# First image's loads spread over three queues, identity products at the start, and one weight's quarters issued by GpSimd

## The chip, the cores and the metric

The kernel runs on one core of a Trainium2 chip. The core has TensorE (PE: matrix products; its weight loads are listed as PEld), VectorE (DVE), ScalarE (ACT), GpSimd (POOL) and SyncE (SP). Each engine works through its own instructions in order. Transfers between memory and the core's buffers are issued by SyncE, ScalarE or GpSimd and carried out by 16 DMA engines. The metric is the device time in microseconds (us) of one execution, the median of several.

## The reference

The input x holds 8 images of 32 x 32 pixels with 512 channels, in float32. Two layers are computed.

1. An attention layer. Each image (1024 tokens of 512 channels) is group-normalized in groups of 16 channels, multiplied by a 512 x 1536 matrix w_qkv to give queries, keys and values, put through softmax attention with 8 heads of 64, multiplied by w_out, and added to x.
2. A deformable attention layer. The result is layer-normalized, projected (wq), put through a 7 x 7 depthwise convolution of stride 2, a GELU and a small projection that gives offsets; at the offset positions the input is sampled bilinearly (256 samples), keys and values are made of the samples by products of weights (wv with mk and mv), the 1024 queries attend to the 256 samples, and an output projection, a layer norm and an MLP with GELU follow.

In the first layer what matters here is:

```python
x_norm = _group_norm(x, gn_scale, gn_bias).reshape(b, seq, c)
qkv = x_norm @ w_qkv + b_qkv
...
out = out @ w_out + b_out
return (x_flat + out).reshape(b, h, w, c)
```

## The kernel before

**Order of the work.** The class `InOrder` keeps every engine's instructions in the order in which the program issues them. That order is written out by hand: `at(place, step)` notes a step with a place, a number in units, and `run_due(until)` issues all noted steps below a place, smallest first. One unit is one tile of 128 queries for one pair of heads: scores, their softmax, and the products with the values. An image has 4 pairs of heads with 8 tiles, so 32 units (`per`); eight images make 256. All instructions of the first layer carry one line in the profile (L54, the helper's), so they are told apart by the names of their tiles.

**The start.** The 8 tiles of the first image, 128 tokens by 512 channels each (256 KB), are loaded before anything else: tiles 0 to 3 by GpSimd, tiles 4 to 7 by SyncE. SyncE then issues three small vectors (gsc, gbi, bqkv, laid onto partitions element by element), the three thirds of w_qkv, 1 MB each, in the order wB (keys), wA (queries), wC (values), and three rows. `norm_steps(0, -100, ...)` notes the first image's steps: `turn(t)` transposes tile t on TensorE by four products with the identity matrix `ident` into a PSUM tile (tag mm, three buffers) and copies it by ScalarE into xT; `two_tiles` takes the statistics of two tiles on VectorE (four instructions); then come the group means, the deviations, a power on GpSimd, the factors, and `norm`, which scales xT in place on VectorE and ScalarE. Between these stand two calls of `warm(3)`, six products of `ident` with xT whose result is not read. Then the first key projection reads wB. After each of the first two transposes, `turn` issues a load of a tile of the next image (`load_x`, two buffers) on GpSimd; w_out is loaded by GpSimd after the first image's normalization, by `load_weight`.

**Scores on their way.** In each unit the exponentials e are transposed by blocks on VectorE into sq; after every second unit `MovedAttention.moved` issues 16 transfers of 128 KB on SyncE that carry sq into et, with the partitions exchanged. Two units later, `part` multiplies et with the values (av). `share` and `spread` send the reciprocal sums through memory and back (rs_d, inv).

**The last image.** Beside the attention of the last image, `fold_steps` multiplies weights of the second layer with each other (wv with mk and mv, wq with mq), and so loads more weights. There is one buffer w of 1 MB for w_out, wq and wv in turn. After wv has been transposed out of it, `load_quarter` fetches w_out for the last image in four quarters of 256 KB at units 25.2, 25.7, 26.2 and 26.7 of that image, issued by ScalarE. Quarters of mv follow at 27.2, 27.9, 28.6 and 29.3 into another buffer (raw), also by ScalarE. The last image's output products (mm<-w,attT) read w_out.

Of the kernel before, what the change touches and what calls it, by code (L numbers as in the profile page):

```python
# [17 lines left out]
P = 128  # L18
# [3 lines left out]
C = 512  # L22
# [4 lines left out]
NQT = QB // P  # L27
NH = 8
HD = 64
# [219 lines left out]
def attention_then_deformable_attention(  # L249
# [30 lines left out]
    nc = tc.nc  # L280
    x_tok = x.rearrange("b h w c -> b (h w) c")
# [8 lines left out]
    ident = const.tile([P, P], F32, tag="ident", name="ident")  # L290
# [7 lines left out]
    def mm_tile():  # L298
        return ps_mm.tile([P, QB], F32, tag="mm", name="mm")

    def by_chunk(w):
        return w.rearrange("(c p) o -> p c o", p=P)
# [6 lines left out]
    def load_cols(pool, v, name):  # L309
        t = pool.tile([P, v.shape[0] // P], F32, tag=name, name=name)  # L310
        with nc.allow_non_contiguous_dma(reason="a vector onto partitions"):
            nc.sync.dma_start(t, v.rearrange("(c p) -> p c", p=P))
        return t

    def load_row(pool, v, name):
        t = pool.tile([P, C], F32, tag=name, name=name)
        nc.sync.dma_start(t, v.partition_broadcast(P))
        return t
# [49 lines left out]
    def at(place, step):  # L368
        due.append((place, len(due), step))
# [40 lines left out]
    def kept(name):  # L410
        return keep.tile([P, NC, C], F32, tag=name, name=name)
# [98 lines left out]
    with ExitStack() as l0:  # L510
# [3 lines left out]
        nc = InOrder(tc)  # L514
        NX = 2
        NX_T = 3
        xs = {}

        def load_x(b, t):
            if b < B:  # L520
                xs[b, t] = work.tile([P, C], F32, tag="x", name="x", bufs=NX)
                nc.gpsimd.dma_start(xs[b, t], x_tok[b][ts(t, P), :])
# [2 lines left out]
        x2 = work.tile([P, NC, QB], F32, tag="xT", name="x2", bufs=NX_T)  # L525
        for t in range(NQT):
            xs[0, t] = work.tile([P, C], F32, tag="attT", name="x0", bufs=NQB * NHP)
            nc.gpsimd.dma_start(xs[0, t], x_tok[0][ts(t, P), :])
            xs[0, NQT + t] = x2[:, t, :]
            nc.sync.dma_start(xs[0, NQT + t], x_tok[0][ts(NQT + t, P), :])  # L530
        w3 = [kept(name) for name in ("wA", "wB", "wC")]
        gsc = load_cols(wp, gn_scale, "gsc")
        gbi = load_cols(wp, gn_bias, "gbi")
        bqkv = load_cols(wp, b_qkv, "bqkv")
        for i in (1, 0, 2):
            nc.sync.dma_start(w3[i], by_chunk(w_qkv)[:, :, ts(i, C)])
        bout = load_row(wp, b_out, "bout")
        room_w = {}

        def load_weight(w):  # L540

            room_w["w"] = work.tile([P, NC, C], F32, tag="w", name="w", bufs=1)
            nc.gpsimd.dma_start(room_w["w"], by_chunk(w))

        def load_quarter(w, c):
            if c == 0:
                room_w["w"] = work.tile([P, NC, C], F32, tag="w", name="w", bufs=1)
            nc.scalar.dma_start(room_w["w"][:, c, :], by_chunk(w)[:, c, :])

        lng_row = load_row(wp, ln_g, "lng_row")  # L550
        lnb_row = load_row(wp, ln_b, "lnb_row")
# [7 lines left out]
            out=g3, in_=g3, pattern=[[-GRP, ng], [0, GRP]], compare_op=ALU.is_ge,  # L559
# [3 lines left out]
            out=g3, in_=g3, pattern=[[GRP, ng], [0, GRP]], compare_op=ALU.is_ge,  # L563
# [5 lines left out]
        def norm_steps(b, start, places):  # L569

            room = {}

            def turn(t):
                blk, i = divmod(t, NQT)
                if i == 0:
                    xTs[b, blk] = work.tile([P, NC, QB], F32, tag="xT", name="xT", bufs=NX_T)
                if t == 0:
                    room["stats"] = work.tile([P, NC, NT // 2, 6], F32, tag="stats", name="stats", bufs=1)
                ps = mm_tile()
                for c in range(NC):  # L580
                    nc.tensor.transpose(ps[:, ts(c, P)], xs[b, t][:, ts(c, P)], ident)
                nc.scalar.copy(xTs[b, blk][:, :, ts(i, P)], ps.rearrange("p (c q) -> p c q", q=P))
                if b > 0:
                    load_x(b + (t + NX) // NT, (t + NX) % NT)
                elif t < NX:
                    load_x(1, t)

            def two_tiles(i):
                blk, half = divmod(i, NQT // 2)
                for c in range(NC):  # L590
                    nc.vector.bn_stats(
                        room["stats"][:, c, i, :], xTs[b, blk][:, c, ts(half, 2 * P)]
                    )


            def gather():
                mv = room["mv"] = work.tile([P, NC, 2], F32, tag="mv", name="mv")
                stats = room["stats"]
                for c in range(NC):
                    nc.vector.bn_aggr(mv[:, c, :], stats[:, c, :, :].rearrange("p s f -> p (s f)"))  # L600

            def means():
                mv = room["mv"]
                ps = mm_tile()
                for m in range(2):
                    half = ds(m * HD, HD)
                    nc.tensor.matmul(
                        ps[half, 0:NC], lhsT=gmat[:, half], rhs=mv[:, :, 0], start=True, stop=True
                    )
                mu = room["mu"] = work.tile([P, NC], F32, tag="mu", name="mu")  # L610
                nc.vector.tensor_copy(mu, ps[:, 0:NC])
                dev = room["dev"] = work.tile([P, NC], F32, tag="dev", name="dev")
                nc.vector.tensor_tensor(dev, mv[:, :, 0], mu, ALU.subtract)
                nc.vector.tensor_tensor(dev, dev, dev, ALU.mult)
                nc.vector.tensor_tensor(dev, dev, mv[:, :, 1], ALU.add)

            def deviations():
                ps = mm_tile()
                for m in range(2):
                    half = ds(m * HD, HD)  # L620
                    nc.tensor.matmul(
                        ps[half, 0:NC], lhsT=gmat[:, half], rhs=room["dev"], start=True, stop=True
                    )
                room["rs"] = work.tile([P, NC], F32, tag="rs", name="rs")
                rstd(room["rs"], ps[:, 0:NC], 1e-6)

            def factors():
                nc.vector.tensor_tensor(room["rs"], room["rs"], gsc, ALU.mult)
                room["add"] = work.tile([P, NC], F32, tag="nadd", name="nadd")
                nc.vector.tensor_tensor(room["add"], room["mu"], room["rs"], ALU.mult)  # L630
                nc.vector.tensor_tensor(room["add"], gbi, room["add"], ALU.subtract)

            def norm(blk):
                xT, add, rs = xTs[b, blk], room["add"], room["rs"]
                for c in range(NC):
                    if b == 0 and c % 2 == 0:
                        nc.vector.tensor_scalar(
                            xT[:, c, :], xT[:, c, :], rs[:, c : c + 1], add[:, c : c + 1],
                            ALU.mult, ALU.add,
                        )  # L640
                    else:
                        nc.scalar.activation(
                            xT[:, c, :], xT[:, c, :], AF.Identity,
                            bias=add[:, c : c + 1], scale=rs[:, c : c + 1],
                        )

            steps = [
                *(lambda t=t: turn(t) for t in range(NT)),
                *(lambda i=i: two_tiles(i) for i in range(NT // 2)),
                gather, means, deviations, factors,  # L650
                *(lambda blk=blk: norm(blk) for blk in range(NQB)),
            ]
            for place, what in zip(places, steps):
                at(start + place, what)
# [352 lines left out]
        def warm(n):  # L1007
            out = mm_tile()
            for c in range(n):
                for m in range(2):  # L1010
                    half = ds(m * HD, HD)
                    nc.tensor.matmul(
                        out[half], lhsT=ident[:, half], rhs=xTs[0, 0][:, 0, :],
                        start=(c == 0), stop=(c == n - 1),
                    )

        norm_steps(0, -100, norm_places)
        for place in (-76.035, -74.5):
            at(place, lambda: warm(3))
        at(-72.5, lambda: load_weight(w_out))  # L1020
        at(-73, lambda: nc.vector.tensor_scalar(bqkv[:, 0:NC], bqkv[:, 0:NC], 1.0 / HD, None, ALU.mult))

# [13 lines left out]
        for b in range(B):  # L1036
# [23 lines left out]
            for hp in range(NHP):  # L1060
                for qt in range(NT):
                    n = first + hp * NT + qt
                    if n % per == 0 and b > 0:
# [9 lines left out]
                    t = qkv[b, hp]  # L1073
# [4 lines left out]
                        at=qt % NQT,  # L1078
# [8 lines left out]
    with ExitStack() as l1:  # L1087
        nc = tc.nc
# [9 lines left out]
        nc = InOrder(tc)  # L1098
# [447 lines left out]
```

## Time and profile before

| | |
|---|---|
| median of 3 runs | 3271.49 us (3262.61 to 3274.84) |
| profiled execution | 3264.03 us, span 3262.3 us |
| mean granted clock of TensorE | 0.998 |
| first transpose on TensorE | at 8.37 us |
| first projection | at 23.04 us |
| last image's quarters of w_out | issued at 2039.54, 2042.22, 2046.60 and 2049.41 us |

The span is the time from the first to the last instruction. In the profile an engine's busy time counts its instructions without waits and without the issuing of transfers; ends of matrix products are modelled. The queue of SyncE is listed as SPq. The chain of work that ended last is followed back from the last instruction, at each step to what released it. In a timeline each row has the start in us, the duration, engine, line, operation, written tile <- read tile, shapes, count, and in brackets the idle time before and what ended it. In a list of waits each row has the waiting engine and group, what it waited for, and the total in us, the number of times and the longest. A wait for several things is put down to the one that came last by the profile; where that one plainly isn't needed by the waiting instruction, it was another.

### The profile page before, as it was taken

Reading aid. Unit: us, or ns where it says so; the run is one execution under the profiler, and the core shown is the slowest. Engines: PE = TensorE matmul, PEld = TensorE weight load, DVE = VectorE, ACT = ScalarE, POOL = GpSimd, SP = SyncE. Lnnn points to the kernel's source line nnn. Section 1 sums busy time; section 2 is a strip of 40 time slices with the busy share of each in tenths; the row PEclk is TensorE's granted clock in tenths of the full one; section 3 lists DMA queues with packets and bytes.
Section 4 is the critical chain, followed back from the end, with each engine's and each line's share of the span. In section 5 each row is a group of like instructions: output and inputs, shape, how many; then the busy total and the mean of one; then the engine's idle time right before and its main releaser. Section 6 shows DMA issues by size and latency. Waiting matters only on the chain.

```text
span 3262.3 us, 59564 instructions
## 1 busy us (share of the span) xinstructions
PE 3217.9 (99%) x21588; PEld 1301.2 (40%) x21588; DVE 2522.9 (77%) x3457; ACT 1780.8 (55%) x3826; POOL 1593.5 (49%) x2026
## 2 busy tenths in 40 slices
PE   8999999999999999999999999999999999999999
PEld 4444344344344444444444434333333333333333
DVE  5776778898888888788788888557868787676765
ACT  3443356566567567557657656335555555554442
POOL 1001316755764665664674577225556565653323
PEclk9999999999999999999999999999999999999999
DMA  5666766777677766676676677678777786887873
GB/s 171 169 179 162 210 181 180 211 200 186 204 196 191 203 197 177 204 211 178 181 223 183 177 216 211 180 228 272 219 240 242 228 264 211 264 259 229 265 236 130
DMA packets 479325, 674.31 MB, mean 207 GB/s; under 512 B 76828, under 2 KB 268632, under 8 KB 478776
## 3 DMA queue, kind: packets, MB, share of 16 engines
q1 hardware_dynamic: 434528, 529.53, 56.8%
q0 software_dynamic: 41136, 136.78, 13.7%
q10 hardware_dynamic: 3368, 4.20, 0.4%
q8 instruction: 171, 2.80, 0.4%
q14 instruction: 122, 1.00, 0.1%
HBM read 263.17 MB, written 138.69 MB: 123 GB/s over the span
## 4 chain that ended last, share of the span: by engine, by line
PE 89%; DVE 3%; ACT 2%; DMA 2%; POOL 1%; issue 1%; SPq 1%; POOLq 0%; DVEq 0%; ACTq 0%
PE mm L54 55%; PE sc L54 17%; PE av L54 17%; ACT e L54 1%; DVE nmax L54 1%; SPq L54 1%; DMA et<-sq_d 1%; DVE sq L54 1%; POOL oa L54 0%; DVE chunk L54 0%; DMA w<-in_L_conv_w_out_dram 0%; DMA sq_d<-sq 0%; POOL xr L54 0%; DMA row<-mid,ii 0%; ACT part_x L54 0%
## 5 line engine op out<-in xcount | busy, mean ns | idle before, releaser
L54 ACT ACTIVATE e<-sc,nmax 128x1024 f32<-128x1024 f32 (+1 forms) x1024 | 803.0, 797 | 531.4 <-DVE nmax L54 524.7
L54 DVE TENSOR_REDUCE nmax<-sc 128x1 f32<-128x1024 f32 (+1 forms) x640 | 750.2, 1212 | 291.3 <-PE sc L54 286.0
L54 POOL TENSOR_TENSOR oa<-part_x,oa 128x256 f32<-128x256 f32 x852 | 639.4, 751 | 542.5 <-ACT part_x L54 496.4
L54 DVE STREAM_TRANSPOSE sq<-e 128x1024 f32<-128x1024 f32 x640 | 764.3, 1225 | 118.5 <-ACT e L54 97.7
L54 ACT ACTIVATE part_x<-pad_x,dww_x 128x256 f32<-128x256 f32 x852 | 441.2, 545 | 259.9 <-POOL oa L54 258.4
L54 PE MATMUL sc<-k,q 64*64 64x512 f32 x4096 | 512.3, 603 | 8.8 <-ACT e L54 6.7
L54 PE MATMUL av<-et,v 128*64 128x256 f32 x4096 | 499.2, 386 | 11.7 <-DMA et<-sq 4.5
L54 PEld LDWEIGHTS av<-et,v 128*64 128x64 f32 x4096 | 273.7, 137 | 328.8 <-issue 162.1
L54 POOL TENSOR_TENSOR mv<-mv,minus_half 128x1 f32<-128x1 f32 x128 | 76.3, 596 | 389.0 <-DVE mv L54 388.0
L54 PEld LDWEIGHTS sc<-k,q 64*64 64x64 f32 x4096 | 137.5, 132 | 314.6 <-issue 208.4
L54 POOL TENSOR_TENSOR chunk<-parts,chunk 128x256 f32<-128x256 f32 x240 | 185.3, 772 | 137.2 <-ACT parts L54 123.2
L54 DVE SCALAR_TENSOR_TENSOR od<-pad_x,dww_x,od 128x256 f32<-128x256 f32 x276 | 232.7, 843 | 5.5
L54 PE MATMUL mm<-wo,attH 128*64 128x512 f32 x1024 | 233.7, 598 | 0.0
L54 PE MATMUL mm<-wC,xT 128*64 128x256 f32 x2048 | 232.1, 379 | 0.0
L54 PE MATMUL mm<-xT,wB 128*64 128x512 f32 x1024 | 230.7, 592 | 0.6 <-DVE xT L54 0.6
L54 PE MATMUL mm<-hat_h,wA 128*64 128x512 f32 x1024 | 230.9, 593 | 0.0
L54 PE MATMUL mm<-xT,wA 128*64 128x512 f32 x1024 | 230.7, 592 | 0.0
L54 PE MATMUL mm<-w,attT 128*64 128x512 f32 x1024 | 230.1, 592 | 0.3 <-DMA w<-in_L_conv_w_out_dram 0.3
L54 PE MATMUL mm<-wm,zT 128*64 128x512 f32 x976 | 220.7, 592 | 0.5 <-ACT zT L54 0.5
L54 ACT ACTIVATION_READ_ACCUMULATOR e<-sc,nmax 128x1 f32 x1024 | 209.1, 204 | 0.0
L54 PEld LDWEIGHTS mm<-wC,xT 128*64 128x64 f32 x2048 | 148.0, 137 | 77.7 <-issue 6.4
L54 PE MATMUL mm<-w,hat_x 128*64 128x512 f32 x768 | 170.2, 593 | 0.0
(198 smaller groups left out, 3457.6 us busy)
## 6 DMA issues: line engine op xcount, KB each, us to landing
et<-sq SPq DMA_DIRECT2D x2048, 128.0 KB
sq_d<-sq SPq DMA_DIRECT2D x128, 512.0 KB
et<-sq_d SPq DMA_DIRECT2D x128, 512.0 KB
inv<-rs_d SPq DMA_DIRECT2D x250, 128.0 KB
xr<-mid POOLq DMA_DIRECT2D x64, 256.0 KB
xr<-in_x_dram POOLq DMA_DIRECT2D x62, 256.0 KB
x<-in_x_dram POOLq DMA_DIRECT2D x60, 256.0 KB
out_dram<-res POOLq DMA_DIRECT2D x60, 256.0 KB
```

The lines of the kernel that those rows point to most:

```text
L54: return self.tc.keep_in_program_order(op(*args, **kwargs))
```

## The change

Five edits. (1) Tiles 0 to 3 of the first image are issued by SyncE, tiles 4 to 7 by GpSimd. (2) SyncE issues only wA and wC behind the small vectors; wB is issued by ScalarE at place -83.54, which is behind its copy of the fourth tile. (3) The first two tiles of the next image are issued by GpSimd at -70, behind w_out, and no longer after the first two transposes' place. (4) `warm_ident(24)` issues 48 products of `ident` with itself (64 by 128 outputs, 24 for each half) ahead of the first transpose; nothing reads their result. (5) The last image's quarters of w_out are issued by GpSimd instead of ScalarE.

```diff
             xs[0, t] = work.tile([P, C], F32, tag="attT", name="x0", bufs=NQB * NHP)
-            nc.gpsimd.dma_start(xs[0, t], x_tok[0][ts(t, P), :])
+            nc.sync.dma_start(xs[0, t], x_tok[0][ts(t, P), :])
             xs[0, NQT + t] = x2[:, t, :]
-            nc.sync.dma_start(xs[0, NQT + t], x_tok[0][ts(NQT + t, P), :])
+            nc.gpsimd.dma_start(xs[0, NQT + t], x_tok[0][ts(NQT + t, P), :])
...
-        for i in (1, 0, 2):
-            nc.sync.dma_start(w3[i], by_chunk(w_qkv)[:, :, ts(i, C)])
+
+        def load_qkv(i, queue):
+            queue.dma_start(w3[i], by_chunk(w_qkv)[:, :, ts(i, C)])
+
+        for i in (0, 2):
+            load_qkv(i, nc.sync)
...
-            nc.scalar.dma_start(room_w["w"][:, c, :], by_chunk(w)[:, c, :])
+            nc.gpsimd.dma_start(room_w["w"][:, c, :], by_chunk(w)[:, c, :])
...
                 if b > 0:
                     load_x(b + (t + NX) // NT, (t + NX) % NT)
-                elif t < NX:
-                    load_x(1, t)
...
+        def warm_ident(n):
+            out = mm_tile()
+            for c in range(n):
+                for m in range(2):
+                    half = ds(m * HD, HD)
+                    nc.tensor.matmul(
+                        out[half, 0:P], lhsT=ident[:, half], rhs=ident,
+                        start=(c == 0), stop=(c == n - 1),
+                    )
+
         norm_steps(0, -100, norm_places)
+        warm_ident(24)
+        at(-83.54, lambda: load_qkv(1, nc.scalar))
         for place in (-76.035, -74.5):
             at(place, lambda: warm(3))
+        for t in range(NX):
+            at(-70, lambda t=t: load_x(1, t))
         at(-72.5, lambda: load_weight(w_out))
```

## The prediction

> **What bounds the kernel now.** I read the page first, then who TensorE waited for, then the start and the place of its longest later wait. Page (busy time; chain by engine):
>
> ```profile
> PE 3217.9 (99%) x21588; PEld 1301.2 (40%) x21588; DVE 2522.9 (77%) x3457; ACT 1780.8 (55%) x3826; POOL 1593.5 (49%) x2026
> ...
> PE 89%; DVE 3%; ACT 2%; DMA 2%; POOL 1%; issue 1%; SPq 1%; POOLq 0%; DVEq 0%; ACTq 0%
> ```
>
> TensorE is busy 3217.9 of 3262.3 us. The idle rest, 44 us, is all that moved loads can win, unless they slow TensorE down. Its waits (who waited for what: total, times, longest):
>
> ```profile
> PE mm L54 <- DMA x<-in_x_dram: 8.4, 1, 8.4
> ...
> PE av L54 <- DVE rs L54: 2.7, 1, 2.7
> ```
>
> The change touches both. The first is the start (timeline: start, duration, what, [idle before]):
>
> ```profile
> 4.46 7.95 SPq L54 DMA_DIRECT2D wB<-in_L_conv_w_qkv_dram  x1
> ...
> 8.37 6.86 PE L54 MATMUL mm<-ident,x 128*128 128x128 f32 x32 [8.37 <-DMA x<-in_x_dram]
> ...
> 12.56 0.59 ACT L54 COPY xT<-mm 128x512 f32<-128x512 f32 x1 [0.27 <-PE mm L54]
> ...
> 13.41 0.59 ACT L54 COPY xT<-mm 128x512 f32<-128x512 f32 x1 [0.27 <-PE mm L54]
> ...
> 14.27 1.64 ACT L54 COPY xT<-mm 128x512 f32<-128x512 f32 x3 [0.27 <-PE mm L54]
> ...
> 14.88 2.71 DVE L54 BATCH_NORM_STATS2 stats<-xT 128x6 f32<-128x256 f32 x8 [0.30 <-ACT xT L54]
> ...
> 23.04 3.65 PE L54 MATMUL mm<-xT,wB 128*64 128x512 f32 x16 [0.64 <-DVE xT L54]
> ```
>
> See that tiles are 0.85 us apart until 14.3 and then 0.55: TensorE is slow for its first 6.0 us. (The granted clock reads 1.00 there, but the durations fall from 475 to 272 ns.) The statistics end at 17.6, and the first projection follows at 23.04. The second place is in the last image of the first layer: SyncE's queue, what it waited for, and TensorE.
>
> ```profile
> 2041.84 1.26 SPq L54 DMA_DIRECT2D et<-sq  x2
> ...
> 2047.55 4.44 SPq L54 DMA_DIRECT2D et<-sq  x6
> ```
> ```profile
> SPq L54 <- DMA w<-in_L_conv_w_out_dram: 4.4, 1, 4.4
> ```
> ```profile
> 2056.48 1.95 PE L54 MATMUL sc<-k,q 64*64 64x512 f32 x16
> 2061.11 2.51 PE L54 MATMUL av<-et,v 128*64 128x256 f32 x16 [2.69 <-DVE rs L54]
> 2063.34 4.84 PE L54 MATMUL mm<-raw 128*64 128x512 f32 x16
> 2068.12 1.95 PE L54 MATMUL sc<-k,q 64*64 64x512 f32 x16
> ```
>
> The view blames a reciprocal, but av reads et, and SyncE moved that et late: it stood 4.4 us waiting for a quarter of w_out that ScalarE had issued. Transfers of SyncE and ScalarE take eight completion counters in turn, and the next user of a counter waits for its last transfer to land. Units come 7.19 us apart (2049.29, 2056.48); the next began at 2068.12, not 2063.66. The price of the stall is thus 4.46 us: 2.69 idle, the rest slow products (granted clock 0.59 and 0.56 in 2062 to 2066).
>
> **The change, part by part.** The sum is made against the profiled execution, 3264.0 us (span 3262.3 and 1.7 around it); the median, 3271.5, is 7.5 above it. Within 0.5% (16 us) a measurement of this kernel can't tell a change from none.
>
> *Quarters of w_out by GpSimd.* ScalarE loses four issues of 0.34 to 0.40 us that lay beside its exponentials and copies: 0. GpSimd gains four of 0.55 (its 256 KB row) to 0.80 (its 1 MB row), 2.2 to 3.2 us, between 2042 and 2048; then it idles 12.6 us. Queued behind them are the share's broadcast (inv, later by 0.55; read at 2056.14, 11.7 us after its issue), three additions of bias and a column, all for later. w_out is first read at 2100.4. So 0 there. What goes is SyncE's wait: the 16 et moves from 2041.84 would be issued by 2051.6 + 0.6 at 0.65 each instead of 2057.6. The late set was used 4.3 us after its last issue began, so the early one is there at 2055.9, against 2058.4 when av wants it. Cover 2.5 us; double traffic on the way may eat some.
>
> What is late next? The quarters of mv stay with ScalarE. The third was issued at 2068.23 after the copy of a product and held SyncE 4.6 us, to 2071.02, which cost nothing. Its product now comes 4.46 earlier: issued 2063.8, landed 2066.6; three more moves and 4.2 us of landing make 2072.8, and av now wants them at 2077.18 - 4.46 = 2072.7. Price 0.1, ends 0 and 4.46 (the stall simply moves there). I take -4.46 + 0.1 = -4.4, ends -4.5 and 0.
>
> The skill speaks against this gain: "DMA: Bandwidth & Descriptors", section "Issuing engines are not separate DMA queues", says that starting transfers from other engines saves only sequencer time. By that alone this part would be worth 0, not -4.4; the row of 4.4 us above is a wait of the issuing queue, and the row decides.
>
> *Identity products.* 48 products of 128 columns go to TensorE once ident exists (GpSimd's select ends at 2.51), before the first transpose. The nearest rows are the warming products: six of 512 columns in 2.79 us, 0.2 of it tail, so 0.86 a pair of halves; at 128 columns 0.214 a pair, 0.43 at half speed. 24 pairs take 5.1 us fast, 10.3 slow. Slow for 6.0 us as today, they do 14 pairs by 8.6, the other 10 in 2.1: transposes begin at 10.7 instead of 8.37, but fast.
>
> The skill's "TensorE: Matmul & The Clock Gate", Part 1, gives about 3.4 us of sustained work until full speed. By that figure the products end at 9.4 and the start would win some 0.5 instead of losing 0.4; this case's row says 6.0 us, and I keep the row.
>
> *Tiles 0 to 3 by SyncE, 4 to 7 by GpSimd.* The landing records show SyncE's four tiles complete at 3.5, 4.1, 9.2 and 9.9, GpSimd's at 8.2, 9.4, 10.5 and 11.2. With the queues exchanged all are there before 10.7 plus 0.55 a tile. From there: first pair of tiles copied at 10.7 + 0.68 + 0.55 + 0.59 = 12.5, then four groups of statistics at 1.36: 18.0, against 17.6. So +0.4. Upper end: all pairs slow, transposes from 12.9, +2.6. Lower end by the next edit.
>
> *wB by ScalarE behind the fourth copy, wA and wC alone on SyncE.* In the built program this issue waits for the counter of gsc, which landed at 12.7: its 512 four-byte pieces stand behind SyncE's tiles. Copies 4 to 7 are queued behind the wait. By my times copy 3 ends at 13.3, after 12.7, and the issue (0.51 as wA's) lies beside it: 0. If tiles come sooner, copies go on at 13.2 at best, statistics end at 17.1: -0.5, the lower end of the whole start. wB landed at 17.3, wA at 20.05, wC at 22.8 in turn; even in the last place wB would be there at 22.8, before 23.04. Its cover is 0.2 to 5 us.
>
> *Next image's two tiles behind w_out on GpSimd.* Two issues of 0.55 move from 5.2 to about 22; the loads and memset behind them shift 1.1 us, and GpSimd then idles 50.7 us. First use is near 93. Price 0.
>
> **Sum:** -4.4 + 0.4 = -4.0: profile about 3260, median 3271.5 - 4.0 = 3267.5.
>
> **The rivals.**
> 1. *The start really gets shorter.* If the products run faster than priced and gsc lands by 10.4, as 15 of its 16 parts did, GpSimd's last tile (11.2) sets the end: copied at 12.5, one group of statistics, 13.9 instead of 17.6, -3.7. Total -8.1: 3263.4. Against it: gsc's last part, at 12.7.
> 2. *The stall moves on.* Another transfer (mv's quarter, or w_out's in a burst) makes the et late all the same; only the start's +0.4 stays: 3271.9. For it: the cover of 0 in the second set.
> 3. *Slower: ScalarE is held by wB's issue.* On SyncE that issue took 7.95 us, since 2560 four-byte pieces were ahead (1 GB/s in 12 to 13 us). If it does the same on ScalarE, copies 4 to 7 wait from 12.7 to 20.7 and the statistics end near 24.6 instead of 18.0. Cost +6.6, total +2.6: 3274.1. It decides once the issue takes over 4 us; against it: the pieces drain by 13.3, and wA's issue then took 0.51.
>
> **How the numbers follow.** Forecast 0.60, rival 1 0.12, rival 2 0.15, rival 3 0.08, others 0.05. The cases lie between 3263.4 and 3274.1; the runs before between -8.9 and +3.4 of their median, of which a new median shows about half. Range 3258 to 3275. No case comes near 16 us: same 0.94, faster 0.03, slower 0.03.
>
> **What would show it.** Right: SyncE has no wait on w_out near 2047, units stay 7.2 us apart and the wait of 2.7 is gone; the first transpose starts between 9.4 and 12.9 at 272 ns; the statistics end between 17.1 and 18.5; ScalarE's issue of wB takes under 1 us. Wrong: a new wait of TensorE on wB after 23, a long gap between copies 3 and 4, a granted clock under 1 in other places, or a later stall as long as the old.

## The result, and the profile after

| | before | after |
|---|---|---|
| median of 12 runs each, same chip | 3266.1 us (3259.9 to 3274.8) | 3276.0 us (3268.9 to 3281.2) |
| profiled execution, and its span | 3264.0, 3262.3 us | 3280.1, 3278.3 us |
| mean granted clock | 0.998 | 0.997 |

The changed kernel is slower: ratio 1.0031, 95% interval 1.0021 to 1.0041, 10 us. The prediction took 0.5% (16 us) for the least that a measurement of this kernel can tell; with 12 executions each the interval is 3 us to either side, so the loss is clear. 4 us were forecast to go, and 3276.0 is above the range of 3258 to 3275.

For this and for every run below I took three lengths from the trace. Their marks are VectorE's score reductions (a unit has two), found in the same order in every kernel. *Stretch*: units 250 to 253, the place of the old stall; three undisturbed units take 21.6 us. *Hand-over*: unit 253 to the first unit of the second layer. *Second layer*: from there to the end of the span.

| us | start to unit 0 | stretch | hand-over | second layer |
|---|---|---|---|---|
| before | 36.4 | 26.0 | 107.2 | 1085.0 |
| after | 36.7 | 25.6 | 114.2 | 1093.7 |

So the start costs what was forecast, the stall is still there, and nearly all the loss lies where the forecast had nothing: 7 us in the hand-over and 9 in the second layer of this execution. Each row is one execution. A second one of the kernel before (the last run below) has 35.0, 26.4, 107.2 and 1086.7, so differences of a microsecond or two in the first and the last column mean nothing.

**The start.** Timeline of the changed kernel (start, duration, engine, what, idle before):

```profile
2.58 7.88 PE L54 MATMUL mm<-ident 128*64 128x128 f32 x96 [2.58 <-POOL ident masks.py:199]
...
10.39 3.95 PE L54 MATMUL mm<-ident,x 128*128 128x128 f32 x32
...
12.19 5.32 DVE L54 BATCH_NORM_STATS2 stats<-xT 128x6 f32<-128x256 f32 x16 [12.19 <-ACT xT L54]
12.43 0.47 ACTq L54 DMA_DIRECT2D wB<-in_L_conv_w_qkv_dram  x1
...
23.43 3.65 PE L54 MATMUL mm<-xT,wB 128*64 128x512 f32 x16 [1.11 <-DVE xT L54]
```

The transposes begin at 10.39 (forecast 10.7) and take 3.95 us instead of 6.86; the statistics end at 17.5; wB's issue takes 0.47 us; the first projection comes at 23.43, 0.39 later than before.

**The old stall.** Waits of SyncE's queue between 2038 and 2075 in the changed kernel (total, times, longest), then TensorE's timeline there:

```profile
SPq L54 <- DVE sq L54: 5.2, 2, 3.6
SPq L54 <- DMA et<-sq: 4.6, 4, 1.9
SPq L54 <- DMA raw<-in_L_conv_mv_w_dram: 4.5, 1, 4.5
```
```profile
2057.27 1.95 PE L54 MATMUL sc<-k,q 64*64 64x512 f32 x16
2061.46 2.80 PE L54 MATMUL av<-et,v 128*64 128x256 f32 x16 [2.24 <-DMA et<-sq]
...
2068.47 1.95 PE L54 MATMUL sc<-k,q 64*64 64x512 f32 x16
```

No wait on w_out is left. But SyncE now waits as long for its own earlier et moves (4.6 us; the 3.6 for sq end at the first of the 16 moves, the 4.5 for raw come after the last). The first move is issued at 2042.64, 0.8 us later than before, but the last at 2057.87, not near the 2051.6 of the prediction, and the next unit starts 4.0 us late (2068.47 instead of 2057.27 + 7.19), where it was 4.46 late before. GpSimd's timeline suggests why the moves land late: the four quarters, 1 MB, come within 5 us, in the middle of the 16 moves (2042.64 to 2057.9). A run below tests this.

```profile
2043.35 0.54 POOL L54 DMA_DIRECT2D w<-in_L_conv_w_out_dram  x1
...
2045.66 0.58 POOL L54 DMA_DIRECT2D w<-in_L_conv_w_out_dram  x1
...
2047.45 1.12 POOL L54 DMA_DIRECT2D w<-in_L_conv_w_out_dram  x2
```

**The hand-over.** The second layer begins with gathers by GpSimd (row<-mid,ii, eight of them), from which VectorE makes smp. Before, GpSimd's timeline (the second gather), then TensorE's:

```profile
2142.41 1.50 POOL L54 DMA_INDIRECT row<-mid,ii  x1 [0.30 <-DVE hat L54]
```
```profile
2161.47 7.02 PE L54 MATMUL mm<-smp,wC 128*64 128x256 f32 x60 [1.08 <-DVE smp L54]
```

After, the same two:

```profile
2150.47 0.98 POOL L54 DMA_INDIRECT row<-mid,ii  x1 [5.99 <-DVE smp L54]
```
```profile
2166.35 9.48 PE L54 MATMUL mm<-smp,wC 128*64 128x256 f32 x60 [4.77 <-DVE smp L54]
```

A new wait of 6.0 us stands before the second gather. TensorE then waits 4.8 us for smp (before 1.1) and, after the idling, does 60 products in 9.48 us (before 7.02) at a granted clock of 0.50 in 2164.8 to 2171.6 (before 1.00 in 2161.5 to 2168.3).

The releaser named (smp) is only the last of several. In the built program the second gather now waits also for the transfer col<-row_b, a bias column of the first layer's last steps; before, it didn't. The tile's listing for col, after:

```profile
L54 ACTq DMA_DIRECT2D col<-row_b x2: 378/382/387, 2131.6 to 2147.6; - x2
...
L54 DVE TENSOR_TENSOR bqq<-col,bqq x1: 164/164/164, 2149.7 to 2149.7; 128x4 f32<-128x4 f32 x1
```

col is issued for the second time at 2147.6 and read by VectorE at 2149.7; 0.6 us after that read has ended the gather goes. Their connection is an address in the built program. Buffers of the first layer lie in the order in which their tags are first used. The change issues the next image's loads later, and with them x's first allocation, so the small buffers that used to follow x now lie before it (bytes in a partition):

| | before | after |
|---|---|---|
| x (2 buffers of 2048, from) | 101248 and 103296 | 109760 and 111808 |
| col (2 buffers, 16 bytes each) | 105408, 105440 | 101312, 101344 |
| second gather's buffer (second layer) | 99456 to 101504 | 99456 to 101504 |

Before, the second gather overwrote x, long out of use. Now it overwrites col, which is still to be loaded and read.

### The profile page after: what moved, and what is told of

Read it like the earlier page. It is cut to its first block, busy times and chain, and to the rows that moved or that the text cites. A ratio compares the mean times of both kernels' runs of the same rounds, so it can differ in the third digit from the quotient of the medians.

```text
span 3278.3 us, 59756 instructions
## 1 busy us (share of the span) xinstructions
PE 3230.1 (99%) x21684; PEld 1307.2 (40%) x21684; DVE 2523.2 (77%) x3457; ACT 1779.7 (54%) x3826; POOL 1594.2 (49%) x2030
## 4 chain that ended last, share of the span: by engine, by line
PE 86%; DVE 3%; DMA 3%; ACT 3%; POOL 2%; issue 1%; SPq 1%; POOLq 0%; ACTq 0%; DVEq 0%
PE mm L54 53%; PE sc L54 17%; PE av L54 16%; ACT e L54 2%; SPq L54 1%; DMA et<-sq_d 1%; DMA et<-sq 1%; DVE nmax L54 1%; DVE sq L54 1%; POOL oa L54 1%; DMA sq_d<-sq 0%; POOL xr L54 0%; DVE chunk L54 0%; ACT part_x L54 0%; DMA row<-mid,ii 0%
```

## The experiments

Theory A: this layout makes the loss. B: the quarters on GpSimd make it, by what they change in queues and counters. C: the start makes it. Ratios are to the kernel before on the same chip, with their 95% interval; 11 or 12 executions against 21 to 35.

**All five edits, old layout.** Only the allocation of the two tiles goes back to its old place:

```diff
-                xs[b, t] = work.tile([P, C], F32, tag="x", name="x", bufs=NX)
+                if (b, t) not in xs:
+                    xs[b, t] = work.tile([P, C], F32, tag="x", name="x", bufs=NX)
...
                 if b > 0:
                     load_x(b + (t + NX) // NT, (t + NX) % NT)
+                elif t < NX:
+                    xs[1, t] = work.tile([P, C], F32, tag="x", name="x", bufs=NX)
```

> All five edits, but the next image's two buffers x are allocated at their old place, in turn, so that the program's buffers lie as before the change (x at byte 101248 of a partition, col at 105408); only their loads stay behind w_out. Theory A (layout: because x is first allocated later, col lies in the bytes of the buffer that the second layer's second gather fills, and GpSimd waits 6 us for col's transfer): no wait of 6.0 us before the second gather, the second layer's first products of samples not 4.8 us late, time about 10 us below the changed kernel: 3264 to 3268, ratio to the kernel before 0.999 to 1.001. Theory B (the quarters of w_out on GpSimd and what they change in queues and counters cause the loss): still about 1.003, 3276. In both the wait for et near 2058 stays, since the four quarters are issued in a burst.

Measured: 1.0014 (1.0005 to 1.0023). Hand-over 107.8, no wait before the second gather. A is right on the place; but the time doesn't return to that of before, and the ratio is above A's 1.001. So A is not all.

**Third edit alone** (the loads and with them the allocation late).

```diff
-                elif t < NX:
-                    load_x(1, t)
...
+        for t in range(NX):
+            at(-70, lambda t=t: load_x(1, t))
```

> The kernel before with the third edit alone: the next image's two tiles are allocated and loaded behind w_out. This gives the buffers the changed kernel's layout (col at 101312, inside the second gather's buffer). Theory A (layout): the wait of about 6 us before the second gather is there and the time is 6 to 11 us above the kernel before, ratio 1.002 to 1.0035. Theory B (quarters) and theory C (start and the queue of wB): no difference, ratio 0.9995 to 1.0005.

Measured: 1.0024 (1.0015 to 1.0033), hand-over 114.2. GpSimd's timeline in this kernel has the wait before the second gather:

```profile
2147.61 0.98 POOL L54 DMA_INDIRECT row<-mid,ii  x1 [7.17 <-DVE smp L54]
```

TensorE waits 4.46 us for smp and takes 9.68 us for the 60 products, as in the changed kernel. The edit that I had priced at 0 makes the whole loss of the hand-over alone.

**Fifth edit alone** (`nc.scalar` to `nc.gpsimd` in `load_quarter`).

> The kernel before with the fifth edit alone: the last image's quarters of w_out are issued by GpSimd. Layout as before. Theory A: SyncE's wait of 4.4 us is gone, but av still comes about 4 us late near 2058 because the quarters, issued in a burst, delay the et transfers themselves; time within 1 us of the kernel before (ratio 0.9995 to 1.0005). Theory B (this edit causes the loss): ratio 1.002 to 1.004. My forecast's own price for this edit was -4.4 us, ratio 0.9987.

Measured: 1.0002 (0.9993 to 1.0011), stretch 26.1, hand-over 107.5. No loss and no gain: B falls, and so does my -4.4.

**Edits 1, 2 and 4 alone.**

> The kernel before with edits 1, 2 and 4 alone: tiles of the first image by the exchanged queues, wB by ScalarE, identity products; layout, quarters and next image's loads as before. Theory A: only the start moves, by -0.5 to +0.6 us, ratio 0.9997 to 1.0003. Theory C (the start, or what its queues shift, causes the loss): ratio 1.002 to 1.004.

Measured: 1.0019 (1.0010 to 1.0028): a loss that A doesn't know. Unit 0 came at 36.0, earlier than before; the hand-over took 107.8; the second layer took 1094.3. So in this trace a start that is not later costs time 2000 us later. The next runs divide this loss.

**Fourth edit alone: 48 identity products.**

> The kernel before with the fourth edit alone: 48 identity products in one PSUM tile ahead of the first transpose. The run of edits 1, 2 and 4 together was 5.6 us slower than before (ratio 1.0019, interval 1.0010 to 1.0028) although its first scores came no later, so one of them costs something beyond the start. Theory D (the one more tile moves every later product on to another of the three PSUM buffers): +3 to +6 us, ratio 1.001 to 1.002, with the loss in the second layer. Theory F (the queues of the loads, edits 1 and 2): at most +2 us from the later first transpose, ratio under 1.0006.

Measured: 1.0018 (1.0008 to 1.0027), second layer 1091.8. TensorE's waits for et in units 260 to 264, before and here (2219 to 2280):

```profile
PE av L54 <- DMA et<-sq_d: 4.0, 2, 2.2
```
```profile
PE av L54 <- DMA et<-sq_d: 6.8, 4, 3.2
```

**The same 48 products over three PSUM tiles.** Against the run above:

```diff
-        warm_ident(24)
+        for _ in range(3):
+            warm_ident(8)
```

> The same 48 identity products, but spread over three PSUM tiles of 16, so that the rotation of the three buffers stands after them where it stood before the change. Theory D: the loss of the run with one tile is gone, ratio 0.9995 to 1.0006. If the products themselves (48 more instructions, the earlier full clock) cost it: as with one tile, +3 to +6 us. Theory F: as with one tile, at most +2 us.

Measured: 1.0007 (0.9998 to 1.0015), second layer 1087.9. The ratio lies between the two expectations, and its interval reaches into both; the trace is not back at before's 1085.0.

**Edits 1 and 2 alone.**

> The kernel before with edits 1 and 2 alone: the first image's tiles by the exchanged queues, wB by ScalarE behind the fourth copy, no identity products. Theory D: no loss, ratio 0.9990 to 1.0005. Theory F: +3 to +6 us, ratio 1.001 to 1.002.

Measured: 1.0002 (0.9993 to 1.0010), second layer 1084.2. No cost of the queues is seen (theory F had 1.001 to 1.002): of the start, the identity products cost the time.

**The changed kernel, col at bytes of its own.**

```diff
-                return work.tile([P, NC], F32, tag="mu", name="col", bufs=2)
+                return work.tile([P, NC], F32, tag="col", name="col", bufs=2)
```

> The changed kernel with the small buffers named col put at bytes of their own (229280), while x stays where the change put it. Theory A (col under the second gather's buffer): the wait of 6.0 us before the second gather is gone, although all five edits and x's new place are kept, and the time falls by 6 to 8 us against the changed kernel, to the level of the run with the old layout: ratio to before 1.0005 to 1.0020. If another part of the new layout costs the time: still 1.0025 to 1.0040.

Measured: 1.0021 (1.0012 to 1.0030), hand-over 108.0. GpSimd's timeline:

```profile
2143.26 1.50 POOL L54 DMA_INDIRECT row<-mid,ii  x1 [0.30 <-issue]
```

Nothing but col's two buffers of 16 bytes moved (to 229280 and 229312; x stays where the change put it), and the wait is gone. This shows the cause of the hand-over's loss. The ratio stands just above what was expected (1.0005 to 1.0020). In the trace 6.2 us of the hand-over are won; in the ratio to before it is 0.0010 here and 0.0017 with the old layout (3 and 6 us), and each ratio is uncertain by 0.0009. The cause is sure, its worth in the median only to some microseconds.

**Pages of instructions.** The list of the DMA queues has rows for instructions. The row of queue 8, before and after:

```profile
q8 instruction: 171, 2.80, 0.4%
```
```profile
q8 instruction: 172, 2.82, 0.4%
```

Each of these packets, pages from here on, is 16384 bytes. TensorE's instruction records (43,933 before) over 171 packets make 257 in each, so I take these for TensorE's, at 256 (64 bytes each): with 256 and with 512 more records in the runs below the count is 172 and 173. A packet takes a DMA engine 1.0 us. Instructions put ahead move all later page limits: near units 260 to 264 the packets start at 2214.9, 2238.4 and 2260.8 before, and with the 48 products alone, counted from the same reduction, at 2223.3, 2245.7 and 2269.1. Theory P: that is how the identity products cost time. Theory D: their PSUM tile does it, since it moves every later product to another of three buffers. In the first of the two expectations that follow, "move every later fetch by 96 instructions" and "128 products are 256 instructions" are wrong: the traces show two matmul records and two weight loads a product, so 48 are 192, three quarters of a page, and 128 are two pages. Whole pages all the same.

```diff
+        warm_ident(64, 16)
```

The first number counts pairs of halves, the second the columns of a product; the change has 24 and 128.

> The kernel before with 128 small identity products (16 columns) in one PSUM tile ahead of the first transpose. The traces show TensorE's instructions arriving in transfers of 16384 bytes, 171 of them for 43,000 instructions, so 256 instructions each; a product and its weight load are two instructions. Theory P (pages: 48 products move every later fetch by 96 instructions, and the fetches then fall on transfers of et that the second layer waits for): 128 products are 256 instructions, a whole page, so the fetches fall where they fell before; the stretch of units 260 to 264 takes 55 to 58 us (before 56.7, with 48 products 57 to 63), ratio 0.9998 to 1.0007. Theory D (one more PSUM tile moves the rotation): as with 48 products, ratio 1.0010 to 1.0022.

Measured: 1.0031 (1.0021 to 1.0040), second layer 1085.4, units 260 to 264 57.1 us. Of the 10 us, 7.1 are the later start (unit 0 at 43.5). The trace fits P. The ratio doesn't: less the start it is about 1.0010, above P's 1.0007 and at the lower end of D's.

**48 narrow products** (`warm_ident(24, 16)`).

> The kernel before with 48 small identity products (16 columns instead of 128) in one PSUM tile: the number of instructions and the rotation of the changed kernel, but a fraction of the work. Theories P and D: the loss is that of the 48 wide products, ratio 1.0010 to 1.0022, the stretch of units 260 to 264 at 57 to 63 us. If the work or the earlier full clock costs the time: ratio 0.9997 to 1.0006.

Measured: 1.0010 (1.0001 to 1.0018), second layer 1089.1, although unit 0 came at 35.0. The trace points to the number of the products or their tile rather than to their work; the ratio, whose interval reaches below 1.0006, doesn't decide.

**Fifth edit alone, quarters spread out.**

```diff
-                at(first + 25.2 + 0.5 * c, lambda c=c: load_quarter(w_out, c))
+                at(first + 26.1 + 1.4 * c, lambda c=c: load_quarter(w_out, c))
```

> The kernel before with the fifth edit, the four quarters of w_out 1.4 units (10 us) apart from place 26.1 on, instead of 0.5. Theory of the burst (the quarters take the DMA engines from the et transfers while they come together): the late et near 2058 is gone, the stretch of units 250 to 253 takes 21.6 to 23 us (three units of 7.19 are 21.6; before 26.0, with the fifth edit alone 26.1), ratio 0.9985 to 0.9995. If the stall stays in another place: 24 us and more there or in the next stretch, ratio 0.9995 to 1.0005.

Measured: 0.9995 (0.9985 to 1.0005), stretch 21.8. GpSimd issued the quarters at 2042.88, 2044.69, 2059.34 and 2063.21: later and in two pairs, not 10 us apart. TensorE's timeline has units 7.2 to 7.4 apart and no late av:

```profile
2053.80 1.95 PE L54 MATMUL sc<-k,q 64*64 64x512 f32 x16
2055.86 1.95 PE L54 MATMUL av<-et,v 128*64 128x256 f32 x16
...
2061.18 1.95 PE L54 MATMUL sc<-k,q 64*64 64x512 f32 x16
```

So it was the burst that made the et late: the stretch is 4.2 us shorter than before. The hand-over grew to 108.9, and the ratio is 1.6 us, within its error of 3.

**Without the four quarters.**

> The kernel before without the four quarters of w_out (the last image's output products then read what is left in that buffer, so this loading is left out of the time). It bounds from below what moving these quarters can win. My forecast's price, 4.4 us: ratio 0.9987, the stretch of units 250 to 253 at 21.6 us. If another transfer makes et late all the same: ratio 0.9993 to 1.0003, the stretch above 23 us.

Measured: 0.9995 (0.9983 to 1.0006), stretch 21.6, hand-over 108.2. Leaving the loads out wins no more in the ratio. Over the eleven traces of this document with the old layout in which ScalarE issues the quarters, stretch and hand-over together take 131.4 to 133.6 us, 132.4 on average; with the quarters spread they take 130.7, without them 129.8. So the traces put a perfect fifth edit at some 2 us, as the ratio does (1.6); the interval, from 5.5 us faster to 2 slower, doesn't exclude 4.4.

**One whole page of narrow products** (`warm_ident(32, 16)`).

> The kernel before with 64 small identity products (16 columns) in one PSUM tile. By the traces one such product is two matmul records and two weight loads (48 products: 96 more matmul records), so 64 are 256 instructions, one whole page, and the 128 of the earlier run were two. Theory P (position in pages): the second layer, from its first scores to the end, takes 1083 to 1087 us as in the kernels without identity products (1083.6 to 1086.1; with 48 products 1087.9 to 1094.3), ratio 0.9993 to 1.0005. Theory D (PSUM rotation): 1088 to 1094 us, ratio 1.0008 to 1.0020.

Measured: second layer 1083.5, as P has it, but ratio 1.0019 (1.0009 to 1.0029), as D has it (P's range ended at 1.0005). The profiled execution (3263.6) was among the shortest of the twelve, whose median was 3269.4. The trace and the median disagree.

**Half a page** (`warm_ident(16, 16)`).

> The kernel before with 32 small identity products, 128 instructions, half a page. Theory D: as with 48 products, second layer 1088 to 1094 us, ratio 1.0008 to 1.0020. Theory P: no whole page, so fetches fall elsewhere than before; it does not say whether half a page is as bad as three quarters: second layer anywhere from 1083 to 1094 us, ratio 0.9995 to 1.0020.

Measured: 1.0016 (1.0007 to 1.0024), second layer 1087.8. Both theories allow it.

**All five edits, with old layout and one whole page** (64 products of 16 columns).

> All five edits, with the two suspected causes undone: x allocated at the old place (its loads stay late), and 64 identity products of 16 columns, one whole page, instead of 48 of 128. If layout and pages are the whole loss: no wait of 6 us before the second gather, hand-over (units 253 to 256) 107 to 109 us, second layer 1083 to 1087 us, ratio 0.9993 to 1.0007. If something else of the change costs time: ratio 1.0010 and more.

Measured: 1.0004 (0.9994 to 1.0015), hand-over 107.4, second layer 1083.8. With both suspected causes undone no loss is seen within the error.

**The same with spread quarters.**

> The same, and the quarters of w_out 1.4 units apart from place 26.1 on. Expected against the run before it: the stretch of units 250 to 253 at 21.6 to 22.5 instead of 24 to 26 us, some 2 to 4 us less in all, ratio to before 0.9982 to 1.0000. If it beats the kernel before, both the change's idea of quarters and its start can be kept.

Measured: 1.0014 (1.0004 to 1.0023); stretch 21.7 as expected, hand-over 112.5. TensorE's timeline:

```profile
2161.58 8.62 PE L54 MATMUL mm<-smp,wC 128*64 128x256 f32 x60 [2.56 <-DVE smp L54]
```

Here the 4 us won are given back: the samples come at 2161.6, hardly earlier than ever (2161.47 before, and units 250 start within 0.7 us of each other), TensorE idles 2.56 us for them, and a granted clock of 0.59 follows in 2161.6 to 2165.0 (60 products in 8.62 instead of 7.02). With the fifth edit alone, spread, and without the quarters this was not so: counted from unit 250 the samples came 2.6 and 3.4 us earlier than before, and TensorE waited 0.9 and 0.8 for them. Why the gathers kept their time here I did not trace. The ratio missed the expectation, and no version is clearly faster than the kernel before.

**One whole page over three PSUM tiles** (44, 10 and 10 products).

> The kernel before with 64 small identity products, one whole page, over three PSUM tiles (44, 10 and 10 products), so that both the pages and the rotation of the PSUM buffers stand as before. Theories P and D together (both cost time): second layer 1083 to 1087 us and ratio 0.9995 to 1.0007. If identity products cost some 5 us in the median whatever their number and tiles: second layer as the trace has it, ratio 1.0010 to 1.0022.

Measured: 1.0005 (0.9996 to 1.0014), second layer 1084.6. The ratio is in the range of P and D together; the interval holds the lower end of the other.

**The kernel before once more.**

> The kernel before, unchanged, run as the changed ones are. Ratio 1.0000 within its interval of about 0.0009; second layer 1083 to 1087 us, hand-over 107 to 109 us; if the ratio is off by more, the small ratios of the other runs are to be read with that error.

Measured: 1.0006 (0.9997 to 1.0015), hand-over 107.2, second layer 1086.7. A difference of 0.0006 between two sets of runs of one kernel is thus to be had for nothing; ratios between 0.9995 and 1.0007 tell no difference here.

**What the identity products' loss is.** By the traces, one execution each, the second layer took 1083.5 to 1086.7 us in the eleven kernels with the old layout and no identity products or whole pages of them (the third edit alone 1087.1), and 1087.8 to 1094.3 in the eight with part of a page. The two sets don't overlap, whatever the PSUM rotation; but the nearest members are 1 us apart, and two executions of the kernel before differ by 1.7.

How it comes about is best seen in units 262 and 263. SyncE writes sq to memory in pairs (sq_d) and reads it back in pairs (et), and the second et waits until the second sq_d has landed. SyncE's timeline before, then after (a row of two runs from the first issue to the end of the second), and TensorE's after:

```profile
2246.22 0.60 SPq L54 DMA_DIRECT2D sq_d<-sq  x1
2247.06 3.07 SPq L54 DMA_DIRECT2D et<-sq_d  x2
```
```profile
2253.66 0.65 SPq L54 DMA_DIRECT2D sq_d<-sq  x1
2254.51 4.35 SPq L54 DMA_DIRECT2D et<-sq_d  x2
```
```profile
2267.92 3.67 PE L54 MATMUL av<-et,vals 128*64 128x512 f32 x6 [4.35 <-DMA et<-sq_d]
```

From the second sq_d to the second et it is 3.54 us before and 4.83 after. In all eight kernels with part of a page a packet of instructions falls into this time, and it lasts 4.8 to 5.3 us (3.9 with half a page). In the twelve others no packet falls there, and it lasts 3.5 us (4.9 in the kernel before once more).

The landing records show the delay itself. A transfer has 16 parts. In the changed kernel the second sq_d's fifteenth part lands at 2257.1 and its last 1.4 us later, and the et is issued 0.05 us after that. So it is, with 1.0 to 1.4 us, in six of the eight; with half a page the last part is 0.4 us late. In the twelve kernels without a packet there it is at most 0.05. Two lengths have another reason: with three PSUM tiles (5.3 us), and in the kernel before once more (4.9), all 16 parts land late, some 5 us after the issue instead of 3.3. Over all sq_d and et transfers of the second layer, in 20 traces, the last part lands on average 1.0 and 1.3 us after the middle one when a packet is under way within 4 us of the issue (532 and 649 transfers), and 0.6 and 0.9 without (1930 and 1688; those with missing records left out).

So a packet delays one part of these transfers, by 0.4 us on average and by 1.3 here, and the delay meets a place where TensorE waits for et: 4.35 us in the changed kernel, none at this unit before. That wait ends with the last part of the second et, which lands 4.3 us after its middle part (0.3 before). Why so late I did not trace.

Not settled is how much of the median this is. One whole page should have cost nothing and measured 1.0019; the run with the rotation kept as well 1.0005, that with all edits and a whole page 1.0004. With the PSUM rotation kept the ratios are 1.0007 and 1.0005, with it moved 1.0004 to 1.0021 (but for the late start), so a second cost by the rotation isn't excluded. The seven kernels with part of a page and without the wait for col measured 1.0007 to 1.0021, 1.0015 on average, some 2 to 7 us. The five with whole pages average 1.0010 (the late start taken off), the five without identity products or the late allocation 1.0000. So by the medians whole pages bring back only a third of the loss, where the traces, one execution each, show all of it back: that identity products cost time is shown, that the place of the pages is the whole reason is not.

## Why the prediction was wrong

- *"Next image's two tiles behind w_out on GpSimd ... Price 0"* is the step that failed most. I costed the issues and their queue, and no cost of theirs is seen (with the loads late and the old layout the hand-over took 107.8). What I left out is that `load_x` allocates as well as loads, so that the step moves buffers: 7.0 us in the hand-over (114.2 against 107.2), shown by the third edit alone (1.0024) and by moving col.
- *"Quarters of w_out by GpSimd"*, -4.4: wrong; the edit alone measured 1.0002. The wait on w_out went, as forecast. But the sum let SyncE issue its 16 moves back to back until 2051.6; the last was issued at 2057.87, because SyncE waited 4.6 us for its own earlier moves while the burst was under way. "Double traffic on the way may eat some" of the cover of 2.5 us: it ate all. That was rival 2, "w_out's in a burst", given 0.15. The ends, -4.5 and 0, held it; I took the wrong one. The size was off too. The stall was read from one trace; in the twelve traces in which ScalarE issues the quarters the stretch takes 23.2 to 26.4 us, 24.7 on average, which is a stall of 3.1. And microseconds won there were taken for won at the end: without any quarters the kernel was 1.6 us faster, and in one run the wait for the samples took all back.
- *"Identity products"*: the start was sized well (10.7 forecast for the first transpose, 10.39 measured), but their price beyond the start was not in the sum: second layer 1091.8 against 1085.0 in the trace, and 2 to 7 us in the median.
- *Start +0.4*: right in size (+0.39), not in its working, and partly by luck. The statistics ended at 17.5, not 18.0; the scaling of xT took back the half microsecond (idle before the first projection 1.11 instead of 0.64). TensorE's slow time was put at 6.0 us, as before; in the six traces with 128-column products it is 3.0 to 6.0, and the first transpose begins at 9.43 to 10.89.
- *wB by ScalarE*: 0, as forecast; rival 3 (issue of 8 us) did not come, 0.47 was measured. Rival 1's condition, gsc by 10.4, nearly came (10.7 by the landing records), but the statistics went on for 5.3 us in a row and set the end.
- *The base*: the median of three runs, 3271.5, was 5.4 above that of twelve. Against 3266.1 the miss in the difference is 14 us, not 8.5.
- Under *"What would show it"*, all signs of the start came out right. The units did not stay 7.2 us apart; and of the signs of being wrong "a later stall as long as the old" came true twice (4.0 us at the old place, 6.0 before the gather) and "a granted clock under 1 in other places" once (0.50 behind the gathers).

## What to carry to other kernels

When a step is moved that allocates as well as loads, write down which buffers change places, and look at the next stage that reuses the bytes: a late, tiny transfer under one of its first buffers holds a whole queue. Time won in front of a chain that runs beside (here the gathers and their sums) is worth what that chain leaves of it, in one run here nothing; read the stall from more than one trace, and cost its removal at the place where the engines next meet. And separate loading from allocating in such an edit: in the run with the old allocation place the loads stayed late and the wait before the gather was gone.

## What the runs showed of the hardware

- Narrow products don't end TensorE's slow first microseconds. Windows of the kernel with 128 narrow products (window, then its length, busy time and records of TensorE): after 13.7 us of 16-column products the transposes still take 191 ns a record for 4.4 us, then 100.

```profile
2.60:16.30 13.70, 13.70 (x256) 13.70 (x256) 0.00 (x0) 0.00 (x0) 3.57 (x10) 1.00 0.99 305
16.40:20.80 4.40, 4.40 (x23) 4.40 (x22) 1.54 (x5) 2.35 (x4) 0.00 (x0) 1.00 1.05 389
20.80:22.10 1.30, 1.30 (x13) 1.14 (x11) 1.30 (x5) 1.20 (x3) 0.00 (x0) 1.00 0.90 332
```

With 128-column products, in the changed kernel, 5.0 us were enough; over the six traces with such products it is 3.0 to 6.0:

```profile
2.60:7.60 5.00, 5.00 (x48) 5.00 (x50) 0.00 (x0) 0.00 (x0) 2.52 (x8) 1.00 0.88 269
7.60:10.40 2.80, 2.80 (x53) 2.63 (x49) 0.00 (x0) 0.00 (x0) 0.00 (x0) 1.00 0.95 235
```

The granted clock reads 1.00 in all five rows. TensorE's slow first microseconds are seen in durations alone.
- Instructions are traffic too: TensorE's came in 171 transfers of 16 KB, one each 19 us, each 1.0 us of a DMA engine. Where one met a 512 KB transfer, a part of that landed up to 1.4 us late, and instructions put ahead move where all later ones fall.
